# A masked attention kernel: the group-0 and group-1 setup in plain order, the last group's scores between its value products

## The chip, the cores and the metric

The kernel runs on one core of a Trainium2 chip. The metric is the device time of one execution in microseconds; the time before is the median of three runs. The profile comes from one further execution of the same program.

## The reference

For each of 128 matrices x[b] (128 nodes by 512 features) two layers are computed, with one 128 by 128 matrix adj for all:

```
h  = relu(layernorm(x))
A  = adj @ h[b]
x  = x + max over features of relu(A[:, None, :] + (A + b0 - A)[:, :, None])   # one number per node
h  = relu(layernorm(x))
q, k, v = h @ Wq + bq, h @ Wk + bk, h @ Wv + bv      # 8 heads of 64
w  = softmax(q k^T / 8 + mask(adj == 0))              # per head
x  = x + w @ v
```

The number that layer 0 adds is the same along a node's features, so that the second layernorm sees the same h; the kernel computes h once.

## The kernel before, in words

**Tiles and groups.** The 128 matrices are taken in 32 groups of 4. For each matrix `m`, `norm(m)` and `norm_end(m)` (lines 249 to 273) compute h in tile `hn`: VectorE (DVE) takes the statistics (`st`, `mv`, `ve`), GpSimd (POOL) the reciprocal deviation (`rstd`, line 264), DVE subtracts the mean and clips (line 269), ScalarE (ACT) scales (line 272), and POOL adds the value bias `bv_sb` to x (line 273). `adjacency(m)` (line 302) is one TensorE product of 512 columns with the transposed adj, and a DVE maximum over it (line 307), which gives the layer-0 number `C`. The transposed h goes to tile `hT` of its group: in groups 0 and 1 by four TensorE transposes and an ACT copy (`transposes`, line 295), in the later groups by a DVE transposition in blocks (`blocks`) and 16 small DMAs (`move`).

**Projections.** q, k and v of a group are computed by Winograd's form of Strassen's method: class `Products` (line 344) has seven methods p1 to p7, each with four matmuls of 256 columns on sums of weight blocks (`s1` to `s4`, made once by `weight_sum`) and of blocks of h (`t1` to `t4`, made by `h_sum`, four DVE instructions a group). Results leave the PSUM banks by ACT (`biased`) or DVE (`add`).

**Attention of one matrix.** `scores(g, i)` (line 471) are 8 products into a PSUM tile `sc` of which there is one, and two exponentials on ACT. `masks(w)` (line 488) are two DVE multiplications. `finish(g, i, w)` (line 492) are 16 products of weights and values into the PSUM tile `pav` (one buffer), whose 65th column is the sum of the weights; then, on DVE, the reciprocal of the sums into `RS`, the multiplication (line 508), and the sum with x and C (line 512); SyncE (SP) issues the output's DMA.

**Order.** Everything inside `tc.manual_schedule()` is ordered by hand. The main loop (lines 556 to 582) runs over the 128 matrices: scores of matrix b, then a share of the products of the next group (`products`, line 455: the last v product p3 of the present group comes in the first share), with masks, the norm of matrix b + 10, and `h_sum` of the group after next dealt in between, then `adjacency` and `finish`. The last group has no products to run beside but its own last one, so its four matrices are worked one after the other.

**The beginning** (lines 524 to 555). The four matrices of group 0 are normalised and transposed. q of group 0 is computed plainly (`plain_q`, 32 matmuls), its first half ahead of the last matrix's transposes. Then follow the 13 products of k and v, and after each product a piece of group 1 or of the first two matrices of group 2: norm and norm_end after one, transposes and adjacency (in the tiles `sc` and `pav`) after the next. Weight sums of k run on DVE, of v and q on POOL. x of group 0 and the weights are loaded in halves on SP's and ACT's queues in turn, x first.

**The end** (lines 585 to 594). After the loop all 1024 reciprocals of each partition are checked against two limits in two DVE passes, the second with a running sum `cnt`; one small product adds the partitions, and the sum goes to `flag`. Each engine loads `flag`, and the program branches to a slow general path if a number is out of range.

Of the kernel before, what the change touches and what calls it, by code (L numbers as in the profile page):

```python
# [36 lines left out]
F32 = mybir.dt.float32  # L41
I32 = mybir.dt.int32
AF = mybir.ActivationFunctionType
ALU = mybir.AluOpType
# [4 lines left out]
G = 4  # L49
# [113 lines left out]
def tile_adj_preln_d2(  # L163
# [36 lines left out]
    def fast(ctx):  # L200
# [6 lines left out]
        ps_sc = ctx.enter_context(tc.tile_pool(name="ps_sc", bufs=1, space=PSUM))  # L207
        ps_av = ctx.enter_context(tc.tile_pool(name="ps_av", bufs=1, space=PSUM))

        X, HN, TB, HT, HB, QT, KT, C, AMAX, WA, RSTD, MV, PR = ({} for _ in range(13))  # L210

        def load(g):
# [5 lines left out]
                )  # L218

        nc.scalar.dma_start(adj_sb, adj)  # L220
        X[0] = xpool.tile([P, G, N], F32, name="xg")
        for i in range(G):
            (nc.sync, nc.scalar)[i % 2].dma_start(X[0][:, i, :], x[i])
        for name, src in (("q", wq), ("k", wk), ("v", wv)):
            for h in range(2):
                (nc.sync, nc.scalar)[h].dma_start(
                    W[name][:, 2 * h : 2 * h + 2, :],
                    src[2 * h * P : (2 * h + 2) * P].rearrange("(c p) f -> p c f", p=P),
                )
        nc.gpsimd.dma_start(b0_sb, b0.rearrange("(p o) -> p o", o=1))  # L230
        nc.gpsimd.dma_start(bq_sb, bq.rearrange("(c p) -> p c", p=P), allow_slow_non_contiguous=True)
        nc.gpsimd.dma_start(bk_sb, bk.rearrange("(c p) -> p c", p=P), allow_slow_non_contiguous=True)
# [9 lines left out]

        pt = ps_mm.tile([P, 512], F32, name="mm")
        nc.tensor.transpose(pt[:, :D], adj_sb, ident)
        nc.scalar.copy(adjT, pt[:, :D])
        nc.vector.tensor_single_scalar(live, adjT, 0.0, op=ALU.not_equal)
        live_h = live.unsqueeze(1).to_broadcast([P, NC, D])

# [45 lines left out]

        def transposes(m):
            g, i = divmod(m, G)
            ph = ps_sc.tile([P, 2, NC, D], F32, name="sc")
            for c in range(NC):
                nc.tensor.transpose(ph[:, 0, c], HN[m][:, c * P : (c + 1) * P], ident)  # L299
            nc.scalar.copy(HT[g][:, i], ph[:, 0])  # L300

        def adjacency(m, pa=None):
            g, i = divmod(m, G)
            if pa is None:
                pa = ps_mm.tile([P, 512], F32, name="mm")
            nc.tensor.matmul(pa, adjT, HN[m], start=True, stop=True)  # L306
            nc.vector.reduce_max(AMAX[g][:, i : i + 1], pa, axis=AX.X)
            if i == G - 1:
                nc.vector.tensor_scalar(C[g], AMAX[g], b0_sb, 0.0, op0=ALU.add, op1=ALU.max)
# [13 lines left out]
                h_quarters(g)  # L323
            nc.vector.tensor_sub(HB[g][o], HB[g][a], HB[g][b])

        def weight_sum(eng, n, k):

            if k == 0:
                w = W[n]
                WA[n] = dict(  # L330
                    a11=w[:, 0:2, 0:HT2], a21=w[:, 0:2, HT2:N],
                    a12=w[:, 2:4, 0:HT2], a22=w[:, 2:4, HT2:N],
                    **{f"s{j + 1}": WS[n][:, j] for j in range(4)},
                )
            o, a, op, b = ("s1 a21 + a22", "s2 s1 - a11", "s3 a11 - a21", "s4 a12 - s2")[k].split()
            eng.tensor_tensor(
                WA[n][o], WA[n][a], WA[n][b], op=ALU.add if op == "+" else ALU.subtract
            )

        def weight_sums(eng, n):  # L340
            for k in range(4):
                weight_sum(eng, n, k)

        class Products:

# [86 lines left out]
                self.mm(self.c, "s4", "b22")  # L432
                self.add(self.dst(0, 1), self.c, self.u2)

        def plain_q(t):

            if t == 0:
                QT[0] = proj.tile([P, NC, T], F32, name="qT")
            h = HT[0][:, 2 * t : 2 * t + 2]
            for f in range(2):  # L440
                bank = ps_mm.tile([P, 2, HT2], F32, name="mm")
                for r in range(2):
                    k = 2 * f + r
                    for c in range(NC):
                        nc.tensor.matmul(  # L445
                            bank[:, r, :], W["q"][:, c, k * P : (k + 1) * P], h[:, :, c],
                            start=r == 0 and c == 0, stop=r == 1 and c == NC - 1,
                            skip_group_check=True,
                        )
                    nc.scalar.activation(  # L450
                        QT[0][:, k, t * HT2 : (t + 1) * HT2], bank[:, r], AF.Identity,
                        bias=bq_sb[:, k : k + 1],
                    )

        def products(g):


# [10 lines left out]
                (k.p3, v.p6, v.p2, v.p7, v.p5, v.p4),  # L468
            )

        def scores(g, i):

            psc = ps_sc.tile([P, 2, NC, D], F32, name="sc")
            for f in range(NC):
                for j in range(2):
                    r = slice(j * HD, (j + 1) * HD)
                    nc.tensor.matmul(  # L477
                        psc[:, j, f, :],
                        KT[g][r, f, i * D : (i + 1) * D],
                        QT[g][r, f, i * D : (i + 1) * D],  # L480
                        start=True, stop=True,
                    )
            w = work.tile([P, 2, NC, D], F32, name="w")
            for j in range(2):
                nc.scalar.activation(w[:, j], psc[:, j], AF.Exp, scale=HD ** -0.5)  # L485
            return w
# [2 lines left out]
            for j in range(2):  # L489
                nc.vector.tensor_tensor(w[:, j], w[:, j], live_h, op=ALU.mult)  # L490

        def finish(g, i, w):
            b = g * G + i
            pav = ps_av.tile([P, 2, 512], F32, name="pav")

            for h in range(H):
                for k in range(2):
                    r = slice(k * HD, (k + 1) * HD)
                    nc.tensor.matmul(  # L499
                        pav[r, h // 4, (h % 4) * HE : (h % 4 + 1) * HE],  # L500
                        w[:, h % 2, h // 2, r], V[g % 2][:, i, h, :],
                        start=True, stop=True,
                    )
            po = pav[:, :, 0 : 4 * HE].rearrange("p k (h e) -> p k h e", e=HE)
            rs = RS[:, b].rearrange("p (k h) -> p k h", k=2)
            nc.vector.reciprocal(rs, po[:, :, :, HD])
            o = work.tile([P, 2, 4, HD], F32, name="o")
            nc.vector.tensor_tensor(  # L508
                o, po[:, :, :, 0:HD], rs.unsqueeze(3).to_broadcast([P, 2, 4, HD]), op=ALU.mult
            )  # L510
            y = o.rearrange("p k h d -> p (k h d)")
            nc.vector.scalar_tensor_tensor(  # L512
                y, X[g][:, i, :], C[g][:, i : i + 1], y, op0=ALU.add, op1=ALU.add
            )
            nc.sync.dma_start(out[b], y)

        with tc.manual_schedule():
            def early(m):

                transposes(m)  # L520
                adjacency(m, ps_av.tile([P, 2, 512], F32, name="pav")[:, 0])


            for m in range(G):
                norm(m)
                norm_end(m)
                if m > 0:
                    early(m - 1)
            plain_q(0)
            early(G - 1)  # L530
            weight_sums(nc.vector, "k")
            for k in range(4):
                h_sum(0, k)
            plain_q(1)
            weight_sums(nc.gpsimd, "v")
            _, k, v = PR[0] = [None] + [Products(0, n) for n in "kv"]
            for s, p in enumerate((
                k.p1, k.p6, k.p2, k.p7, k.p5, k.p4, v.p1, k.p3, v.p6, v.p2, v.p7, v.p5, v.p4,
            )):
                p()  # L540
                m = G + s // 2
                if m < 2 * G + 2:
                    if s % 2 == 0:
                        norm(m)
                        norm_end(m)
                    elif m < 2 * G:
                        early(m)
                    else:
                        blocks(m)
                        adjacency(m, ps_av.tile([P, 2, 512], F32, name="pav")[:, 0])  # L550
                if s >= 4 and s % 2 == 0 and s < 12:
                    weight_sum(nc.gpsimd, "q", s // 2 - 2)
                if s >= 8 and s < 12:
                    h_sum(1, s - 8)
            move(2 * G + 1)
            for b in range(B):
                g, i = divmod(b, G)
                m = b + 2 * G + 2
                if i == 0 and g + 3 < NG:
# [22 lines left out]
                    move(m)  # L582


            ok = work.tile([P, 2, NC, D], F32, name="w").rearrange("p j f d -> p (j f d)")
            cnt = stat.tile([P, 1], F32, name="cnt")
            rs_all = RS.rearrange("p b h -> p (b h)")
            nc.vector.tensor_single_scalar(ok, rs_all, SUM_LO, op=ALU.is_ge)
            nc.vector.scalar_tensor_tensor(
                ok, rs_all, SUM_HI, ok, op0=ALU.is_le, op1=ALU.mult, accum_out=cnt  # L590
            )
            pc = ps_mm.tile([P, 512], F32, name="mm")
            nc.tensor.matmul(pc[0:1, 0:1], cnt, ones, start=True, stop=True)
            nc.vector.tensor_copy(flag, pc[0:1, 0:1])

    with ExitStack() as c:
        fast(c)
# [35 lines left out]
```

## Time and profile before

| | us |
|---|---|
| median of 3 runs (1621.72 to 1622.07) | 1621.97 |
| profiled execution, its own time | 1621.72 |
| its span, first to last instruction | 1620.0 |
| TensorE busy | 1586.6 |
| VectorE busy | 1114.2 |
| ScalarE busy | 422.9 |
| GpSimd busy | 259.6 |
| first scores start (after the beginning) | 74.97 |
| last product of the last v starts | 1595.60 |
| flag written | 1617.2 |

How to read it: the span is divided into the beginning, up to the first scores, the main loop, and the end, from the scores of the last matrix but four. Busy time counts instructions in execution, and a wait is idle time with a releaser in brackets behind the instruction that ends it. In the timeline each row has the start, the duration, engine, line, operation, output and inputs, and the count of merged instructions; an fp32 matmul has two records.

### The profile page before, as it was taken

Reading aid. Unit: us, or ns where it says so; the run is one execution under the profiler, and the core shown is the slowest. Engines: PE = TensorE matmul, PEld = TensorE weight load, DVE = VectorE, ACT = ScalarE, POOL = GpSimd, SP = SyncE. Lnnn points to the kernel's source line nnn. Section 1 sums busy time; section 2 is a strip of 40 time slices with the busy share of each in tenths; the row PEclk is TensorE's granted clock in tenths of the full one; section 3 lists DMA queues with packets and bytes.
Section 4 is the critical chain, followed back from the end, with each engine's and each line's share of the span. In section 5 each row is a group of like instructions: output and inputs, shape, how many; then the busy total and the mean of one; then the engine's idle time right before and its main releaser. Section 6 shows DMA issues by size and latency. Waiting matters only on the chain.

```text
span 1620.0 us, 29469 instructions
## 1 busy us (share of the span) xinstructions
PE 1586.6 (98%) x11819; PEld 1319.8 (81%) x11819; DVE 1114.2 (69%) x2044; ACT 422.9 (26%) x844; POOL 259.6 (16%) x278
## 2 busy tenths in 40 slices
PE   6899999999999999999999999999999999999996
PEld 4688888888888888888888888888888888888885
DVE  3576777766777767777767777667777677777655
ACT  2322222222222222222222222222222222222221
POOL 4311111111111111111111111111111111111000
PEclk9999999999999999999999999999999999999999
DMA  4033222232222232222332222322222322223201
GB/s 164 1 72 73 68 60 51 69 75 69 63 46 70 69 79 65 67 44 69 72 73 68 54 56 69 76 68 64 47 69 69 79 65 67 44 69 73 47 27 40
DMA packets 299082, 104.02 MB, mean 64 GB/s; under 512 B 264448, under 2 KB 264576, under 8 KB 298944
## 3 DMA queue, kind: packets, MB, share of 16 engines
q1 hardware_dynamic: 297520, 99.69, 25.5%
q8 instruction: 94, 1.54, 0.4%
q10 hardware_dynamic: 1248, 2.16, 0.4%
q14 instruction: 44, 0.36, 0.1%
q0 software_dynamic: 176, 0.27, 0.1%
HBM read 37.03 MB, written 33.55 MB: 44 GB/s over the span
## 4 chain that ended last, share of the span: by engine, by line
PE 97%; DVE 1%; ACT 1%; issue 0%; DMA 0%; POOL 0%; ACTq 0%; DVEq 0%; POOLq 0%
PE mm L372 72%; PE pav L499 9%; PE sc L477 8%; PE mm L306 6%; PE mm L445 1%; PE pav L306 1%; PE sc L299 0%; DVE w L490 0%; DMA xg<-in_x_dram 0%; ACT hn L272 0%; DVE o L512 0%; DVE o L508 0%; POOL rstd L264 0%; DVE st L259 0%; ACT qT L450 0%
## 5 line engine op out<-in xcount | busy, mean ns | idle before, releaser
L264 POOL TENSOR_TENSOR rstd<-ve,mhalf 128x1 f32<-128x1 f32 x128 | 84.3, 659 | 1225.9 <-DVE ve L262 1087.6
L485 ACT ACTIVATE w<-sc 128x512 f32<-128x512 f32 x256 | 138.9, 595 | 515.4 <-PE sc L477 515.4
L499 PEld LDWEIGHTS pav<-v,w 128*64 128x64 f32 x4096 | 130.3, 137 | 99.6 <-issue 54.4
L372 PE MATMUL mm<-hs,sq_sb 128*128 128x256 f32 x744 | 179.0, 383 | 0.0
L372 PE MATMUL mm<-hs,sk_sb 128*128 128x256 f32 x768 | 176.4, 379 | 0.0
L372 PE MATMUL mm<-sv_sb,hs 128*128 128x256 f32 x768 | 176.2, 379 | 0.0
L273 POOL TENSOR_TENSOR xg<-xg,bv_sb 128x512 f32<-128x512 f32 x128 | 162.9, 1273 | 35.2 <-DVE hn L269 27.5
L490 DVE TENSOR_TENSOR w<-w,live 128x512 f32<-128x512 f32 x256 | 164.7, 685 | 1.0 <-ACT w L485 1.0
L372 PEld LDWEIGHTS mm<-sv_sb,hs 128*128 128x128 f32 x768 | 145.9, 190 | 20.7 <-issue 1.0
L272 ACT ACTIVATE hn<-hn,rstd 128x512 f32<-128x512 f32 x128 | 92.9, 726 | 267.7 <-DVE hn L269 206.3
L372 PEld LDWEIGHTS mm<-hs,sk_sb 128*128 128x128 f32 x768 | 145.9, 190 | 20.3 <-issue 0.5
L372 PEld LDWEIGHTS mm<-hs,sq_sb 128*128 128x128 f32 x744 | 138.8, 190 | 21.4
L499 PE MATMUL pav<-v,w 128*64 128x65 f32 x4096 | 148.5, 224 | 6.7 <-DVE w L490 6.7
L477 PE MATMUL sc<-qT,kT 64*128 64x128 f32 x2048 | 148.7, 285 | 0.0
L420 DVE TENSOR_TENSOR u<-mm,p1b 128x512 f32<-128x512 f32 x63 | 43.5, 691 | 128.3 <-PE mm L372 128.3
L477 PEld LDWEIGHTS sc<-qT,kT 64*128 64x128 f32 x2048 | 124.2, 187 | 9.1 <-issue 0.3
L372 PE MATMUL mm<-hT,wk_sb 128*128 128x256 f32 x512 | 124.2, 385 | 0.0
L372 PE MATMUL mm<-wv_sb,hT 128*128 128x256 f32 x512 | 120.9, 379 | 0.0
L306 PE MATMUL mm<-hn,adjT 128*128 128x512 f32 x236 | 120.5, 592 | 0.0
L372 PE MATMUL mm<-hT,wq_sb 128*128 128x256 f32 x496 | 120.4, 386 | 0.0
L372 PEld LDWEIGHTS mm<-wv_sb,hT 128*128 128x128 f32 x512 | 97.3, 190 | 13.7 <-issue 0.5
L372 PEld LDWEIGHTS mm<-hT,wk_sb 128*128 128x128 f32 x512 | 94.7, 190 | 15.8 <-issue 0.5
(84 smaller groups left out, 2033.1 us busy)
## 6 DMA issues: line engine op xcount, KB each, us to landing
out_dram<-o SPq DMA_DIRECT2D x128, 256.0 KB, 2.1
xg<-in_x_dram SPq DMA_DIRECT2D x62, 512.0 KB, 5.1
hT<-tb SPq DMA_DIRECT2D x960, 32.0 KB, 2.0
xg<-in_x_dram SPq DMA_DIRECT2D x2, 256.0 KB, 3.4
xg<-in_x_dram ACTq DMA_DIRECT2D x2, 256.0 KB, 5.6
wq_sb<-in_L_gnn_Wq_dram SPq DMA_DIRECT2D x1, 512.0 KB, 7.9
wk_sb<-in_L_gnn_Wk_dram SPq DMA_DIRECT2D x1, 512.0 KB, 11.1
wq_sb<-in_L_gnn_Wq_dram ACTq DMA_DIRECT2D x1, 512.0 KB, 10.6
```

Source lines behind the costliest of these rows:

```text
L264: nc.gpsimd.tensor_tensor(rstd, ve, mhalf, op=ALU.pow)
L272: nc.scalar.activation(HN[m], HN[m], AF.Copy, scale=RSTD[m])
L273: nc.gpsimd.tensor_tensor(X[g][:, i, :], X[g][:, i, :], bv_sb, op=ALU.add)
L306: nc.tensor.matmul(pa, adjT, HN[m], start=True, stop=True)
L372: nc.tensor.matmul(bank[:, r, :], lhs, rhs, start=first and r == 0 and c == 0, stop=r == 1 and c == 1, skip_group_check=True,)
L420: nc.vector.tensor_tensor(self.u3, self.b, self.pf[1], op=ALU.add)
L445: nc.tensor.matmul(bank[:, r, :], W["q"][:, c, k * P : (k + 1) * P], h[:, :, c], start=r == 0 and c == 0, stop=r == 1 and c == NC - 1, ski ...
L477: nc.tensor.matmul(psc[:, j, f, :], KT[g][r, f, i * D : (i + 1) * D], QT[g][r, f, i * D : (i + 1) * D], start=True, stop=True,)
L485: nc.scalar.activation(w[:, j], psc[:, j], AF.Exp, scale=HD ** -0.5)
L490: nc.vector.tensor_tensor(w[:, j], w[:, j], live_h, op=ALU.mult)
L499: nc.tensor.matmul(pav[r, h // 4, (h % 4) * HE : (h % 4 + 1) * HE], w[:, h % 2, h // 2, r], V[g % 2][:, i, h, :], start=True, stop=True,)
```

## The change

It does two things. The beginning: x of group 0 is loaded by `load(0)` on SP in two transfers, each weight matrix in one transfer of 1 MB on ACT. The copy of the transposed adj moves from ACT to DVE. `plain_q` goes; q of group 0 is computed by `Products` as in all groups, and its weight sums run on DVE, those of k and v on POOL. The work of a group stands together: four matrices, `h_sum`, and for group 0 then all 20 products of q, k, v but the last; group 1's norms, transposes and adjacencies follow after these, then the two matrices of group 2. Transposes and adjacencies use the tile `mm` of the products.

The end: the main loop stops five matrices early. The last matrix of group 30 and the four of group 31 follow by hand, with the scores of group 31 between the last v products. Two of the weight tiles and one tile `pav` come from buffers that are free by then (`spare`). The check of the reciprocals is made in two parts by `count`: one over the first 124 matrices behind `finish` of matrix 3 of group 30, one over the last four at the end, whose small products add up in one PSUM tile.

```diff
-        X[0] = xpool.tile([P, G, N], F32, name="xg")
-        for i in range(G):
-            (nc.sync, nc.scalar)[i % 2].dma_start(X[0][:, i, :], x[i])
+        load(0)
         for name, src in (("q", wq), ("k", wk), ("v", wv)):
-            for h in range(2):
-                (nc.sync, nc.scalar)[h].dma_start(
-                    W[name][:, 2 * h : 2 * h + 2, :],
-                    src[2 * h * P : (2 * h + 2) * P].rearrange("(c p) f -> p c f", p=P),
-                )
+            nc.scalar.dma_start(W[name], src.rearrange("(c p) f -> p c f", p=P))
...
-        nc.scalar.copy(adjT, pt[:, :D])
+        nc.vector.tensor_copy(adjT, pt[:, :D])
...
         def transposes(m):
-            ph = ps_sc.tile([P, 2, NC, D], F32, name="sc")
+            ph = ps_mm.tile([P, NC, D], F32, name="mm")
...
-        def adjacency(m, pa=None):
+        def adjacency(m):
             g, i = divmod(m, G)
-            if pa is None:
-                pa = ps_mm.tile([P, 512], F32, name="mm")
+            pa = ps_mm.tile([P, 512], F32, name="mm")
...
+        def spare_tile():
+
+            t = proj.tile([P, NQ, 2, NC, Q], F32, name="tb")
+            return t.rearrange("p a i c r -> p (a i c r)")
+
-        def scores(g, i):
+        def scores(g, i, spare=False):
...
-            w = work.tile([P, 2, NC, D], F32, name="w")
+            if spare:
+                w = spare_tile().rearrange("p (j f d) -> p j f d", j=2, f=NC)
+            else:
+                w = work.tile([P, 2, NC, D], F32, name="w")
...
-            pav = ps_av.tile([P, 2, 512], F32, name="pav")
+            if spare:
+                pav = ps_sc.tile([P, 2, NC, D], F32, name="sc").rearrange("p j f d -> p j (f d)")
+            else:
+                pav = ps_av.tile([P, 2, 512], F32, name="pav")
...
+        def count(b0, b1):
+
+            r = RS[:, b0:b1].rearrange("p b h -> p (b h)")
+            ok = spare_tile()[:, 0 : (b1 - b0) * H] if b0 == 0 else live[:, 0 : G * H]
+            cnt = stat.tile([P, 1], F32, name="cnt")
+            nc.vector.tensor_single_scalar(ok, r, SUM_LO, op=ALU.is_ge)
+            nc.vector.scalar_tensor_tensor(
+                ok, r, SUM_HI, ok, op0=ALU.is_le, op1=ALU.mult, accum_out=cnt
+            )
+            if b0 == 0:
+                PC.append(ps_mm.tile([P, 512], F32, name="mm"))
+            nc.tensor.matmul(PC[0][0:1, 0:1], cnt, ones, start=b0 == 0, stop=b1 == B)
...
-            for m in range(G):
-                norm(m)
-                norm_end(m)
-                if m > 0:
-                    early(m - 1)
-            plain_q(0)
-            early(G - 1)
-            weight_sums(nc.vector, "k")
-            for k in range(4):
-                h_sum(0, k)
-            plain_q(1)
-            weight_sums(nc.gpsimd, "v")
-            _, k, v = PR[0] = [None] + [Products(0, n) for n in "kv"]
-            for s, p in enumerate((
-                k.p1, k.p6, k.p2, k.p7, k.p5, k.p4, v.p1, k.p3, v.p6, v.p2, v.p7, v.p5, v.p4,
-            )):
-                p()
-                m = G + s // 2
-                if m < 2 * G + 2:
-                    if s % 2 == 0:
-                        norm(m)
-                        norm_end(m)
-                    elif m < 2 * G:
-                        early(m)
-                    else:
-                        blocks(m)
-                        adjacency(m, ps_av.tile([P, 2, 512], F32, name="pav")[:, 0])
-                if s >= 4 and s % 2 == 0 and s < 12:
-                    weight_sum(nc.gpsimd, "q", s // 2 - 2)
-                if s >= 8 and s < 12:
-                    h_sum(1, s - 8)
+            for g in (0, 1):
+                for m in range(g * G, g * G + G + 1):
+                    if m < g * G + G:
+                        norm(m)
+                        norm_end(m)
+                    if m > g * G:
+                        transposes(m - 1)
+                        adjacency(m - 1)
+                for k in range(4):
+                    h_sum(g, k)
+                if g == 0:
+                    weight_sums(nc.vector, "q")
+                    weight_sums(nc.gpsimd, "k")
+                    weight_sums(nc.gpsimd, "v")
+                    PR[0] = q, k, v = [Products(0, n) for n in "qkv"]
+                    for p in (
+                        q.p1, q.p6, q.p2, q.p7, q.p5, q.p4, k.p1, k.p6, q.p3, k.p2, k.p7,
+                        k.p5, k.p4, v.p1, k.p3, v.p6, v.p2, v.p7, v.p5, v.p4,
+                    ):
+                        p()
+            for m in (2 * G, 2 * G + 1):
+                norm(m)
+                norm_end(m)
+                blocks(m)
+                adjacency(m)
             move(2 * G + 1)
-            for b in range(B):
+            for b in range(B - G - 1):
...
-            ok = work.tile([P, 2, NC, D], F32, name="w").rearrange("p j f d -> p (j f d)")
-            cnt = stat.tile([P, 1], F32, name="cnt")
-            rs_all = RS.rearrange("p b h -> p (b h)")
-            nc.vector.tensor_single_scalar(ok, rs_all, SUM_LO, op=ALU.is_ge)
-            nc.vector.scalar_tensor_tensor(
-                ok, rs_all, SUM_HI, ok, op0=ALU.is_le, op1=ALU.mult, accum_out=cnt
-            )
-            pc = ps_mm.tile([P, 512], F32, name="mm")
-            nc.tensor.matmul(pc[0:1, 0:1], cnt, ones, start=True, stop=True)
-            nc.vector.tensor_copy(flag, pc[0:1, 0:1])
+            g = NG - 1
+            k3, v6, v2, v7, v5, v4 = parts[G - 1]
+            w = scores(g - 1, G - 1)
+            k3()
+            masks(w)
+            v6()
+            w0 = scores(g, 0)
+            v2()
+            masks(w0)
+            finish(g - 1, G - 1, w)
+            count(0, B - G)
+            v7()
+            w1 = scores(g, 1)
+            v5()
+            masks(w1)
+            w2 = scores(g, 2, spare=True)
+            v4()
+            w3 = scores(g, 3, spare=True)
+            finish(g, 0, w0)
+            masks(w2)
+            PR[g][2].p3()
+            finish(g, 1, w1)
+            masks(w3)
+            finish(g, 2, w2, spare=True)
+            finish(g, 3, w3)
+            count(B - G, B)
+            nc.vector.tensor_copy(flag, PC[0][0:1, 0:1])
```

## The prediction

> **What bounds the kernel now.** I read the page first (engines, the 40 slices, the chain of work that ended last), then the busy time by stretch, then the timelines of the first 75 us and of the last 40 us.
>
> ```profile
> PE 1586.6 (98%) x11819; PEld 1319.8 (81%) x11819; DVE 1114.2 (69%) x2044; ACT 422.9 (26%) x844; POOL 259.6 (16%) x278
> PE   6899999999999999999999999999999999999996
> PE 97%; DVE 1%; ACT 1%; issue 0%; DMA 0%; POOL 0%; ACTq 0%; DVEq 0%; POOLq 0%
> ```
>
> The busy time of one stretch, the columns being stretch, length, then PE, PEld, DVE, ACT, POOL, clock, DMA share and GB/s:
>
> ```profile
> 118.90:1536.00 1417.10, 1417.10 (x10622) 1182.73 (x10620) 1002.82 (x1837) 374.19 (x750) 220.56 (x229) 1.00 0.27 65
> ```
>
> TensorE is full from 75 us to 1597 us: in the stretch of 1417.10 us it is busy 1417.10. The change leaves that loop alone, so only the two ends can move. Of TensorE's 33 us of idle time some 20 lie before 75 us and some 13 after 1597.6 us.
>
> The beginning, from the timeline (start, duration, then the work):
>
> ```profile
> 8.56 1.91 PE L306 MATMUL pav<-hn,adjT 128*128 128x512 f32 x2
> 12.11 1.26 POOL L273 TENSOR_TENSOR xg<-xg,bv_sb 128x512 f32<-128x512 f32 x1 [6.42 <-DVE mv L260]
> 15.34 1.11 PE L299 MATMUL sc<-ident,hn 128*128 128x128 f32 x4 [4.87 <-ACT hT L300]
> ...
> 44.89 0.68 DVE L259 BATCH_NORM_STATS2 st<-xg 128x6 f32<-128x512 f32 x1
> ...
> 46.06 0.73 POOL L264 TENSOR_TENSOR rstd<-ve,mhalf 128x1 f32<-128x1 f32 x1 [6.88 <-DVE ve L262]
> 46.76 1.26 POOL L273 TENSOR_TENSOR xg<-xg,bv_sb 128x512 f32<-128x512 f32 x1
> 46.82 0.72 ACT L272 ACTIVATE hn<-hn,rstd 128x512 f32<-128x512 f32 x1
> ...
> 47.60 0.66 PE L299 MATMUL sc<-ident,hn 128*128 128x128 f32 x4
> ...
> 48.09 1.02 PE L306 MATMUL pav<-hn,adjT 128*128 128x512 f32 x2
> ```
>
> The chain from the statistics to the transposes runs over three engines and takes 47.60 - 44.89 = 2.71 us. Here it lies beside products. POOL's 6.42 us before 12.11 are put down to DVE, which had long been done; what came last is the load of `bv_sb` (issued at 3.50, 8.5 us to landing). It holds the second `rstd`, hence the second matrix.
>
> The end:
>
> ```profile
> 1613.12 0.21 DVE L506 RECIPROCAL RS<-pav 128x8 f32<-128x8 f32 x1 [1.14 <-PE pav L499]
> 1613.37 0.69 DVE L508 TENSOR_TENSOR o<-pav,RS 128x512 f32<-128x512 f32 x1
> 1614.16 0.75 DVE L512 SCALAR_TENSOR_TENSOR o<-xg,c,o 128x512 f32<-128x512 f32 x1
> 1614.83 0.69 DVE L588 TENSOR_SCALAR w<-RS 128x1024 f32<-128x1024 f32 x1
> 1615.55 1.22 DVE L589 SCALAR_TENSOR_TENSOR w<-RS,w 128x1024 f32<-128x1024 f32 x1
> 1616.70 0.08 DVE L589 DVE_READ_ACCUMULATOR w<-RS,w 128x1 f32 x1
> 1616.84 0.09 PEld L593 LDWEIGHTS mm<-ones,cnt 128*1 128x1 f32 x2 [3.90 <-DVE w L589]
> ```
>
> From the last value product to the count's matmul it is 3.72 us, all DVE, while TensorE waits. The clock column shows what an idle TensorE costs:
>
> ```profile
> 1613.00:1613.20 0.20, 0.08 (x4) 0.00 (x0) 0.07 (x1) 0.00 (x0) 0.00 (x0) 1.00 0.00 0
> 1613.40:1613.60 0.20, 0.00 (x0) 0.00 (x0) 0.20 (x1) 0.00 (x0) 0.00 (x0) 0.50 0.00 0
> ```
>
> [...] 0.50 at 1613.3, and in the first 19 us an adjacency (two records) takes 1.71 us in the chain against 0.86 later, four transposes 1.11 against 0.65. [...] the trace shows no matmul out of the written order. [...] Here the loads keep them at 380 to 390 GB/s until about 20 us, so dealing x and weights over two queues moves an order, not the total.
>
> **The change part by part: beginning.** Written order per engine is kept in the hand-ordered part; I count on that. Times are from the span's start, a product (4 matmuls, 8 records) is 1.73 us.
>
> Group 0 as now up to the second matrix, because `bv_sb` still gates it. Its landing is the unknown: between 5.7 us (POOL would not stop: -6.4) and 20 us (end of all loads: +8); I take 12.1 again, the bytes being the same. With the weights alone on ACT's queue and x alone on SP's, each x pair lands later than now by an estimate of 1 to 3 us; the second pair is first read at 11 us, so that is hidden. The adjacency's transpose is copied on DVE (0.24 us, DVE idle there): nothing. Transposes into an `mm` bank no longer wait for the copy `hT` at 14.72: the second starts at 14.87 instead of 15.34 (-0.47). The fourth matrix's normalisation ends at 20.99, its transposes and adjacency at 22.55.
>
> q.p1 then runs to 24.28. q.p6 needs t2 and s2, and on DVE these stand behind one another: reduction and c 0.87, four `h_sum` 2.53, two weight sums 1.33 (from 30.12 to 36.05 now), so 22.60 + 4.73 = 27.33. TensorE idles 3.1 us. From 27.37, 19 products take 32.8: E = 60.2. (Plain q was 32 matmuls, Winograd's 28; that is in the sum.) The k and v sums on POOL end at about 31.6, before they are read.
>
> Group 1's norms, until now between these products, stand in DVE's queue behind the last eviction. From E: eviction 0.65, chain 2.71, transposes and adjacency 1.51: 4.87. The third matrix waits for the first's reduction: 0.64 + 2.64 + 1.51 = 4.79. The fourth comes 2.17 later, paced by POOL (0.7 + 1.27 each). Reduction, c and four `h_sum`: 3.32. Matrix 8: 2.77 + 0.86 = 3.63; its reduction 0.64; matrix 9: 3.63. Sum 23.05: the first scores start at 83.25, now 75.04. **+8.2 us** at full clock. Nothing covers this stage: no products are left to run in it. The loads and moves for later groups stay in place relative to the scores.
>
> **End.** I count from t = 0, the scores of matrix 3 of group 30 (1581.78 now). Scores 1.09, k.p3, v.p6, scores(31,0) 1.09, v.p2, finish 1.08: TensorE ends at 8.45; DVE is through with the masks by 8.2. Then count(0, 124). Its matmul is written before v.p7, so v.p7 and all behind it wait for reciprocal, two output steps and two passes over 992 numbers: 3.72 us less 0.05, plus 0.2 for itself. v.p7 starts at 12.45. Then v.p7, scores(31,1), v.p5, scores(31,2), v.p4, scores(31,3) to 20.91, finish(31,0) to 21.99, v.p3 to 23.72. The exponentials fit between the scores in one `sc` buffer (1.1 us against 1.73). From 22.05 DVE sets the end: three output steps 1.64, masks 1.24, v.p3's sum 0.65, steps 1.7, masks 1.24, steps 1.7 and 1.7, short count 0.5, matmul and flag 0.45: about 33.0. Now the flag is written at 35.43: **-2.4 us**. The gain without the stall would be 6.2. Unknown is whether the last output's landing (2.0 us after issue) shows beyond the program's last 2.8 us: 0 to +0.9; I take 0.
>
> **Clock restarts.** One restart cost 1.85 us at the start now (0.46 + 0.85 + 0.20 + 0.34 over the four pieces from 15.34 to 20.22). New idle stretches: before q.p6 3.1 us ([...] half, 0.9); E to the first transposes 3.4 us (1.3 on the chain); matrix 8 after 6 us idle (0.85); matrix 9 with the scores behind it (1.85); v.p7 after 3.8 us idle (1.85). Together **+6.75**, from 0 to about 12.
>
> Sum: 8.2 - 2.4 + 6.75 = +12.55. On the profiled run's 1621.72 (span 1620.0 and 1.7 around it) that is 1634.3; on the median of the three runs, 0.25 higher, 1634.5.
>
> **Rivals.**
> - The clock holds: [...] the end's rounds with 1.68 us idle in 4.15 kept 1.00. For it: those rounds. Against: 0.50 came at once [...]. 8.2 - 2.4: 1627.8.
> - More waits: group 1's stage stays at half clock (about +3), `bv_sb` lands later (+2), the finish of matrix 1 waits for v.p3's sum because it takes V as a whole (+2). For it: nothing in the stage fills TensorE over half. Against: nothing in the trace asks for all three. 1641.5.
> - The count's matmul holds nothing (another order): -6.2 in place of -2.4 and no restart there: 1628.9. Against: program order.
> - Faster than before: DVE does not keep the written order and starts group 1's norms in its idle time beside group 0's products. The stage of 23.05 would shrink to its matmuls, 7.8 us: -15.2, and its restarts (4.0) go: 1615.3. It decides once some 13 of these 19 us are taken in. For it: one copy written ahead of the ordered part (`adjT`, 7.50) ran behind a later normalisation on ACT. Against: inside that part every DVE and POOL instruction stands as written.
>
> **How the numbers follow.** Forecast 0.65, clock holds 0.13, more waits 0.12, count holds nothing 0.06, faster 0.04. The range, 1626.5 to 1641, takes in the forecast's restarts from nothing to about 12 us, the cases of the held clock and of the count, and reaches to the edge of the case of more waits. 0.2% is 3.2 us, about what can be told from no change: faster 0.04, same 0.04 (low ends of the clock and count cases), slower 0.92.
>
> **What would show it.** First scores at 83 to 88 us; products closed up from 27 to 60; transposes of group 1 after 60 with TensorE half idle and the clock at 0.50 in places; in the end a TensorE idle of 3.7 us released by the count's DVE pass, and slower v.p7. It is wrong if group 1's statistics run before 55 us, if the second matrix is released much before 14 us, or if the first scores come before 80.

## The result, and the profile after

The changed kernel takes 1644.08 us, median of 4 runs (1642.44 to 1644.41), beside 1622.02 us for the kernel before: the ratio is 1.0134, 95% interval [1.0117, 1.0152]. It is slower, as forecast, but by 22 us where the forecast had 12.5. The profiled execution took 1644.07 us, its span is 1642.2.

From the page of the changed kernel: TensorE's share and instructions among the engines, then its busy tenths and its clock, also in tenths, in the 40 slices.

```profile
PE 1592.8 (97%) x11813; PEld 1322.6 (81%) x11813; DVE 1124.5 (68%) x2053; ACT 421.3 (26%) x841; POOL 262.4 (16%) x278
PE   4879999999999999999999999999999999999997
PEclk8989999999999999999999999999999999999998
```

TensorE has six instructions fewer than before and is busy 6.2 us longer, so part of its work ran slowly. The slices that lost are the first and the third, 6-8-9 before and 4-8-7 now, and the clock, at 9 in every slice before, is 8 in both.

| us | before | after | difference |
|---|---|---|---|
| first scores start | 74.97 | 96.39 | +21.42 |
| from there to the scores of matrix 3 of group 30 | 1506.81 | 1507.50 | +0.69 |
| from there to the flag | 35.28 | 35.15 | -0.13 |
| from there to the end of the span | 2.94 | 3.16 | +0.22 |
| span | 1620.0 | 1642.2 | +22.2 |

So nearly all of it is in the beginning. The 0.69 us behind it are the first scores themselves, which took 1.87 us in place of 1.16. The timeline of the beginning after the change, in rows of start, duration, engine, line, operation, output and inputs:

```profile
24.71 0.68 DVE L317 TENSOR_TENSOR hs<-hT 128x512 f32<-128x512 f32 x1
...
26.98 1.74 DVE L317 TENSOR_TENSOR hs<-hT 128x512 f32<-128x512 f32 x1
28.14 1.70 POOL L324 TENSOR_TENSOR sv_sb<-wv_sb 128x512 f32<-128x512 f32 x1
...
33.87 3.75 PE L358 MATMUL mm<-hs,sq_sb 128*128 128x256 f32 x8 [8.85 <-DVE sq_sb L325]
...
70.52 0.68 DVE L253 BATCH_NORM_STATS2 st<-xg 128x6 f32<-128x512 f32 x1
...
73.22 0.66 PE L293 MATMUL mm<-ident,hn 128*128 128x128 f32 x4 [3.34 <-ACT hn L266]
...
88.89 2.07 PE L299 MATMUL mm<-hn,adjT 128*128 128x512 f32 x2 [6.21 <-ACT hn L266]
```

Two things are to be seen. q.p6 waits 8.85 us for a weight sum of DVE, and the DVE passes ahead of it last 1.74 us, though the first of the same kind took 0.68. POOL's passes beside them last 1.70 us, and the two engines start theirs in turn. And group 1's transposes and adjacencies, which in the kernel before lay between products, stand alone behind them, most of them with a wait for the normalisation.

The busy time by stretch, in the columns of the prediction, for the stretch of q.p6 and q.p2 and for group 1's stage:

```profile
33.80:40.40 6.60, 6.53 (x17) 5.30 (x18) 2.89 (x3) 0.00 (x0) 1.05 (x1) 0.54 0.00 0
69.90:96.40 26.50, 11.66 (x30) 4.33 (x30) 16.79 (x37) 6.34 (x10) 11.45 (x12) 0.77 0.00 1
```

In the first TensorE is full, but its granted clock is 0.54, and q.p6 and q.p2 take 6.49 us where two products at full clock take 3.46: nearly half of this time is lost to the clock. In the second it has 11.66 us of work in 26.50, at a clock of 0.77.

The end of the changed kernel, from its timeline:

```profile
1616.52 0.19 PE L505 MATMUL mm<-ones,cnt 128*1 128x1 f32 x2 [3.71 <-DVE tb L500]
1616.64 3.63 PE L358 MATMUL mm<-sv_sb,hs 128*128 128x256 f32 x8
```

The first count's small product waits 3.71 us for DVE, v.p7 stands behind it, and then v.p7 takes 3.63 us in place of 1.9, at a granted clock of 0.57 (1616.3 to 1620.3).

### The profile page after: what moved, and what is told of

Same layout as the page of the kernel before. It is cut to its first block, busy times and chain, and to the rows that moved or that the text cites. A ratio compares the mean times of both kernels' runs of the same rounds, so it can differ in the third digit from the quotient of the medians.

```text
span 1642.2 us, 29462 instructions
## 1 busy us (share of the span) xinstructions
PE 1592.8 (97%) x11813; PEld 1322.6 (81%) x11813; DVE 1124.5 (68%) x2053; ACT 421.3 (26%) x841; POOL 262.4 (16%) x278
## 4 chain that ended last, share of the span: by engine, by line
PE 94%; issue 3%; DVE 1%; POOL 1%; ACT 0%; DMA 0%; DVEq 0%; POOLq 0%; ACTq 0%
PE mm L358 70%; PE sc L448 9%; PE pav L476 8%; PE mm L299 7%; DMA xg<-in_x_dram 0%; ACT hn L266 0%; PE mm L293 0%; POOL rstd L258 0%; DVE o L485 0%; DVE amax L300 0%; DVE st L253 0%; DVE o L489 0%; DVE hs L317 0%; DVE tb L464 0%; POOL xg L267 0%
## 5 line engine op out<-in xcount | busy, mean ns | idle before, releaser
L358 PE MATMUL mm<-hs,sq_sb 128*128 128x256 f32 x768 | 186.4, 386 | 8.9 <-DVE sq_sb L325 8.9
L358 PEld LDWEIGHTS mm<-hs,sq_sb 128*128 128x128 f32 x768 | 144.4, 191 | 31.6 <-issue 9.2
L299 PE MATMUL mm<-hn,adjT 128*128 128x512 f32 x256 | 136.1, 614 | 9.6 <-ACT hn L266 9.6
L358 PE MATMUL mm<-hT,wq_sb 128*128 128x256 f32 x512 | 125.4, 388 | 0.0
L300 DVE TENSOR_REDUCE amax<-mm 128x1 f32<-128x512 f32 x128 | 86.1, 673 | 53.7 <-PE mm L299 52.9
L358 PEld LDWEIGHTS mm<-hT,wq_sb 128*128 128x128 f32 x512 | 95.7, 192 | 16.3 <-issue 0.5
```

The source lines that it names most:

```text
L358: nc.tensor.matmul(bank[:, r, :], lhs, rhs, start=first and r == 0 and c == 0, stop=r == 1 and c == 1, skip_group_check=True,)
```

## The experiments

Times are compared with runs of the kernel before on the same chip, whose medians lay between 1622.5 and 1623.1, so "+14.2" means 14.2 us over that. Single runs of the kernel before lay between 1620.95 and 1626.27, so a difference in the medians under about 1 us says nothing. The changed kernel stands at +22.1 in this count. The expectations name kernels by their time or by a short name: e1_sums_apart is the first below, e2_end_alone the end alone, e4_total_late the changed kernel with the first count's product moved.

**The two engines' sums apart.** In the changed kernel POOL's k and v sums wait, by one small addition, for DVE's last q sum.

```diff
                     weight_sums(nc.vector, "q")
+                    gate = stat.tile([P, 1], F32, name="ve")
+                    nc.gpsimd.tensor_tensor(
+                        gate, WS["q"][:, 3, 1, N // 2 - 1 : N // 2], mhalf, op=ALU.add
+                    )
                     weight_sums(nc.gpsimd, "k")
```

> The changed kernel, with one tiny POOL addition put ahead of POOL's k and v weight sums that reads the last of DVE's q weight sums, so that POOL's sums run after DVE's instead of beside them. [...] DVE's sums of two SBUF tensors and POOL's take turns while both run, and that alone makes the six DVE passes between 24.7 and 33.7 us cost 8.9 instead of 3.9 us; apart, the passes take 0.68 each, q.p6 starts at 28.3 to 28.8 instead of 33.87, and the time falls by 5 to 6.5 us, to 1637.5 to 1639. Rival operands: the passes are slow because of what they read (hT just written, weight blocks); then they stay at 1.7 us and the time at 1644.

Measured 1637.25 us, +14.2, ratio 1.0085 [1.0067, 1.0103]; first scores at 89.18. Its timeline, a DVE pass, q.p6 and the first pass of POOL:

```profile
25.20 0.68 DVE L317 TENSOR_TENSOR hs<-hT 128x512 f32<-128x512 f32 x1
...
27.96 2.80 PE L358 MATMUL mm<-hs,sq_sb 128*128 128x256 f32 x8 [3.26 <-DVE sq_sb L325]
...
29.24 1.26 POOL L324 TENSOR_TENSOR sk_sb<-wk_sb 128x512 f32<-128x512 f32 x1
```

All eight DVE passes are back at 0.68 to 0.69 and POOL's at 1.26 to 1.27, and the wait at q.p6 is 3.26 us, near the 3.1 that the prediction had. Delaying POOL's work by 7 us made the kernel 7 us faster. The sizes fit passes that take turns: the 1.74 us of a DVE pass are its own 0.68 and most of one of POOL's, 1.26. That the two engines slow each other is shown here; why they do, no run tests.

**The same collision put into the kernel before.** There POOL's v sums ran from 21.89 to 26.94 beside matmuls, and DVE's eight passes from 30.99. A like addition makes POOL start with DVE.

```diff
+            gate = stat.tile([P, 1], F32, name="ve")
+            nc.gpsimd.tensor_tensor(gate, C[0][:, 0:1], mhalf, op=ALU.add)
             weight_sums(nc.gpsimd, "v")
```

> The kernel before with POOL's v weight sums held back, by a tiny POOL addition ahead of them that reads C of group 0, until DVE makes its k weight sums and h sums (31 to 36 us): the disputed collision by itself. [...] DVE's eight passes of 0.68 and POOL's four of 1.26 alternate, about 1.7 us for each pair while POOL has work; DVE is through at 40 to 41 instead of 36.05, the norm of matrix 4 and k.p6 follow later, and the time rises by 2 to 4.5 us. Rival operands: passes stay at 0.68, time unchanged.

Measured 1623.0 us, +0.5, ratio 1.0001 [0.9991, 1.001]. The timeline:

```profile
37.28 1.72 POOL L336 TENSOR_TENSOR sv_sb<-wv_sb,sv_sb 128x512 f32<-128x512 f32 x1
37.79 1.75 DVE L324 TENSOR_TENSOR hs<-hT 128x512 f32<-128x512 f32 x1
39.58 0.69 DVE L324 TENSOR_TENSOR hs<-hT,hs 128x512 f32<-128x512 f32 x1
```

The slowing appears in another kernel with other tiles and goes in the pass after POOL's last one. DVE was through 5.3 us later (41.39 instead of 36.05), 1.0 of it because the whole chain began later in this profile (31.15 instead of 30.12), and the time didn't rise: plain q's products ran meanwhile, and k.p6, which reads the sums, was not held. The transposes of matrix 4 waited 0.87 us in place of 0.54, and the first scores, at 76.40, were 1.4 us later than before, of which 1.0 was there from the start. So the slowing is confirmed and its expected price is not: the collision cost time where someone waited for the sums (8.85 us at q.p6 in the changed kernel, 3.26 with the sums apart), and none that can be told where nobody did (+0.5 here).

**Group 1 laced between products again,** in the changed kernel.

```diff
+                p()
+                t = s - 2
+                m = G + t // 2
+                if 0 <= t and m < 2 * G + 2:
+                    if t % 2 == 0:
+                        norm(m)
+                        norm_end(m)
+                    elif m < 2 * G:
+                        early(m)
...
+                if 8 <= t < 12:
+                    h_sum(1, t - 8)
```

> The changed kernel with the norms, transposes, adjacencies and sums of group 1 and of matrices 8 and 9 dealt between group 0's products again, as the kernel before deals them (from q.p2 on, with its PSUM tiles); loads, Winograd q, weight sums and the end as changed. Theory: the stage of 26.6 us between the last v product and the first scores goes and leaves its 7.8 us of matmuls: first scores at about 77.5 instead of 96.4, time 1644.1 - 18.8 = 1625.3, or up to 3 more where a norm comes late for its place. Rival: the stage is mostly work that TensorE has to do anyway; then under 10 us are gained, 1634 or more.

Measured 1633.14 us, +10.1, ratio 1.0057 [1.0039, 1.0075]; first scores at 84.90. That lies between the two forecasts: the first scores are 11.5 us earlier, not 18.8. The transposes and adjacencies now wait for their norms, with 1.62, 0.54, 2.09, 1.75 and 1.68 us of idle TensorE, and the collision is still whole, with q.p6 at 33.25:

```profile
33.25 3.75 PE L359 MATMUL mm<-hs,sq_sb 128*128 128x256 f32 x8 [8.85 <-DVE sq_sb L326]
...
60.49 0.66 PE L513 MATMUL sc<-ident,hn 128*128 128x128 f32 x4 [2.09 <-ACT hn L266]
```

**Both cures at once,** the two edits above in one kernel. Six matrices are laced, not the eleven of the expectation: the four of group 1 and matrices 8 and 9.

> The changed kernel with both cures of its beginning: POOL's k and v weight sums held back until DVE's q sums are through, and the eleven matrices of group 1 interleaved with group 0's products as before. Theory "two separate losses" (the sums of the two engines slow each other, 6.8 us when taken alone; the unlaced beginning leaves TensorE short and idle, 11 us when taken alone): they add, 1644.1 - 6.8 - 11 = 1626.3 us, first scores at about 78. Rival "one loss seen twice" (with the order laced, the late norms set the pace whichever way the sums go): no better than the laced order alone, 1633 us, first scores at about 85.

Measured 1633.93 us, +11.4, ratio 1.0068 [1.0051, 1.0084]; first scores at 87.03. The rival's number: all that the parted sums had brought is lost again. The timeline of this kernel shows where it went:

```profile
31.63 0.15 DVE L256 TENSOR_SCALAR ve<-mv 128x1 f32<-128x1 f32 x1
...
38.27 1.26 POOL L328 TENSOR_TENSOR sv_sb<-wv_sb,sv_sb 128x512 f32<-128x512 f32 x1
39.49 0.55 POOL L258 TENSOR_TENSOR rstd<-ve,mhalf 128x1 f32<-128x1 f32 x1
...
40.08 0.72 ACT L266 ACTIVATE hn<-hn,rstd 128x512 f32<-128x512 f32 x1 [7.49 <-POOL rstd L258]
...
40.85 1.11 PE L513 MATMUL sc<-ident,hn 128*128 128x128 f32 x4 [7.42 <-ACT hn L266]
```

The held sums are a block of 10.3 us on POOL, and the reciprocal deviation of matrix 4, ready to be worked out at 31.78, stands behind it until 39.49. The profile names ACT as the releaser of TensorE's 7.42 us; ACT was waiting for POOL.

**The sums dealt out behind the norms.**

```diff
-            weight_sums(nc.gpsimd, "k")
-            weight_sums(nc.gpsimd, "v")
...
+                if t in (0, 2):
+                    weight_sums(nc.gpsimd, "k", (t, t + 1))
+                if t in (4, 6, 8, 10):
+                    weight_sums(nc.gpsimd, "v", (t // 2 - 2,))
```

> The kernel with both cures (1633.9 us, first scores 87.03), with POOL's eight k and v sums dealt out behind the norms of group 1 rather than in one block ahead of them. Theory "the block on POOL holds the reciprocal deviation of matrix 4 from 31.8 to 39.5, so TensorE waits 7.4 us": that wait goes, first scores at 77 to 79, 1624 to 1626 us; the two cures add after all. Rival "late norms set the pace in any case": first scores at 84 to 87, 1631 to 1634 us.

Measured 1624.89 us (12 runs, 1621.97 to 1628.25), +2.0, ratio 1.0007 [0.9997, 1.0016], no longer told from the kernel before.

```profile
28.68 3.75 PE L364 MATMUL mm<-hs,sq_sb 128*128 128x256 f32 x8 [2.75 <-DVE sq_sb L329]
...
34.32 0.72 POOL L258 TENSOR_TENSOR rstd<-ve,mhalf 128x1 f32<-128x1 f32 x1 [4.31 <-DVE ve L256]
...
36.24 1.26 POOL L327 TENSOR_TENSOR sk_sb<-wk_sb 128x512 f32<-128x512 f32 x1
...
36.98 0.64 PE L518 MATMUL sc<-ident,hn 128*128 128x128 f32 x4
```

First scores came at 80.21 in the profiled execution, a little behind the 77 to 79 expected; it was the slowest of the 12, and in it q.p6 and q.p2 ran slowly (3.75 and 3.19 us, where the previous kernel's profile has 1.97 and 1.89; the first slice of its clock is at 8 tenths, there at 9). The deviation of matrix 4 no longer stands behind the sums, and its transposes start without a wait, which settles it: the two losses add, and the block on POOL had hidden it. Of the 22 us, some 8 go with the parted sums and some 12 more with the lacing.

**The clock kept up.** On the kernel with the sums apart, products of 512 columns that nobody reads are added in TensorE's idle stretches.

```diff
+            def keep(n):
+                t = ps_av.tile([P, 2, 512], F32, name="pav")
+                for _ in range(n):
+                    nc.tensor.matmul(t[:, 0], ident, W["q"][:, 0, :], start=True, stop=True)
...
+                        if p == q.p1:
+                            keep(4)
+                    keep(3)
...
+                keep(6 if m == 2 * G else 3)
```

> The kernel of e1_sums_apart with products that nobody reads (identity by a weight slice, 512 columns, 0.86 us each, into the idle tile pav) put into TensorE's idle stretches of the beginning: 4 behind q.p1, 3 behind v.p4, 6 ahead of matrix 8's adjacency, 3 ahead of matrix 9's. They fit in the idle time, so they only keep the clock up. Theory restarts: at half clock the beginning loses 1.8 us at q.p6 and q.p2, about 1.3 at group 1's first matrices, 0.85 at each of the adjacencies of matrices 8 and 9, 0.7 at the first scores: 5.5 below e1_sums_apart (1637.25), 1631.8. Rival: the stage of group 1 is paced by DVE, ACT and POOL alone; then only q.p6, q.p2 and the scores gain, 2.5 us, 1634.7.

Measured 1634.33 us, +11.8, ratio 1.0064 [1.0047, 1.0082]. First scores at 83.45, 5.73 earlier than without, 1.2 of it from an earlier q.p1. q.p6 took 1.96 us in place of 2.80, the adjacencies of matrices 8 and 9 1.12 in place of 2.07, the first scores 1.16 in place of 1.72, and the third slice of the clock is at 9 tenths in place of 8. So the restarts in the beginning were worth some 4.5 us. Group 1's stage took 23.7 us. The whole gained only 2.4 us: from the last count's product to the end of the span it was 6.3 us instead of 3.4. The waits and the page of this kernel show where:

```profile
SPq L636 <- PEq L607: 2.9, 1, 2.9
...
q8 instruction: 95, 1.56, 0.4%
```

SyncE's queue waits 2.9 us for TensorE's queue at the branch on `flag` (line 607), and q8, which the profile lists as an instruction queue, has 95 packets where it has 94 in the kernel before, the changed one and the one with the sums apart. This loss lies behind the last matmul (1624.99), so it isn't one of matmuls at a lower clock; whether the branch waited for that packet isn't shown. The total thus agrees with the rival's 1634.7 by luck; the 4.5 us ahead of the scores fit the theory, which had 4.8 there (5.5 less the 0.7 of the scores themselves).

**The loads alone,** in the kernel before.

```diff
-            (nc.sync, nc.scalar)[i % 2].dma_start(X[0][:, i, :], x[i])
+        load(0)
...
+            nc.scalar.dma_start(W[name], src.rearrange("(c p) f -> p c f", p=P))
```

> The kernel before with the changed kernel's loads of x of group 0 and of the weights (two transfers of x on SP, three of 1 MB on ACT), nothing else. Theory: bv_sb lands about 0.9 us later, as in the trace after (POOL's first addition at 13.00 instead of 12.11), and that shifts all behind it: +0.9, first scores at 75.9. Rival: the plain q products hide it, 0; or q waits for the one large transfer of wq (12.3 us to landing from 1.21, so 13.5, ahead of the products at 20): 0 too.

Measured 1623.07 us, +0.5, ratio 0.9999 [0.9992, 1.0006]. POOL's first use of `bv_sb` came at 12.42 and the first scores at 75.14, 0.2 us later than before. The way x and the weights are dealt over the queues costs nothing that can be told.

**The end alone,** the new end behind the old beginning.

```diff
-            for b in range(B):
+            for b in range(B - G - 1):
...
+            finish(g - 1, G - 1, w)
+            count(0, B - G)
+            v7()
```

> The beginning of the kernel before with the new end. Theory: the end is worth nothing as it stands (from the scores of matrix 3 of group 30 to the flag 35.15 us in the trace after, 35.28 before), so the time is 1621.9, within 0.5 of before, and the whole +22 is the beginning's. Rival: a part of the loss is the end's (the clock restart behind the count is larger than it looks), 1624 or more.

Measured 1623.29 us, +0.2, ratio 0.9995 [0.9986, 1.0004]: as expected nothing.

**The first count's product moved behind the last scores,** DVE's counting left in place, in the changed kernel.

```diff
-            count(0, B - G)
+            cnt = count(0, B - G)
...
             w3 = scores(g, 3, spare=True)
+            total(cnt, 0, B - G)
```

> The changed kernel with the first count's small matmul moved behind the last scores; the DVE passes stay where they are. Theory: the 3.7 us in which v.p7 waits for that matmul and the restart of 1.9 us behind it go, 1644.1 - 5.5 = 1638.6. Rival: DVE sets the end anyway, its passes being ahead of the evictions that v.p5 and the masks need; then 2 us or less, 1642 or more.

Measured 1638.24 us, +15.2, ratio 1.0088 [1.0071, 1.0105]. The timeline shows v.p7 at its own pace and the product with no wait:

```profile
1612.03 1.99 PE L358 MATMUL mm<-sv_sb,hs 128*128 128x256 f32 x8
...
1621.07 0.19 PE L508 MATMUL mm<-ones,cnt 128*1 128x1 f32 x2
```

The last count came 6.14 us earlier than in the changed kernel, 0.58 of it from its beginning: the stall with its restart is worth 5.6 us.

**That end with the old beginning.**

> The beginning of the kernel before, the new end, and the first count's small matmul moved behind the last scores: both repairs in one. Theory: as e4_total_late against the changed kernel (1638.24 against 1644.08), 5.8 us below e2_end_alone: 1617.3, and below the kernel before by 5.5. Rival: [...] the gain is under 3 us.

Measured 1617.3 us (1616.72 to 1617.92), -5.2, ratio 0.9957 [0.994, 0.9973]: faster than both kernels. Two more edits go on from there.

```diff
+        nc.gpsimd.dma_start(bv_sb, bv.rearrange("(o f) -> o f", o=1).to_broadcast([P, N]))
         nc.gpsimd.dma_start(b0_sb, b0.rearrange("(p o) -> p o", o=1))
...
-        nc.gpsimd.dma_start(bv_sb, bv.rearrange("(o f) -> o f", o=1).to_broadcast([P, N]))
```

> The beginning of the kernel before with the end's count held behind the last scores (1617.3 us), and in it the bias column bv_sb loaded first on POOL's queue instead of last. Theory "the place in the queue sets when it lands": bv_sb lands at 7 to 9 us instead of 12, the second matrix's chain and everything behind it 4 to 4.5 us earlier, 1613 us. Rival [...] it lands as late as before, first scores at 75 to 76, 1617 us. Worse if the columns now landing later (the other biases, the mask) hold the first matrix.

Measured 1613.3 us (1612.59 to 1614.03), -9.2, ratio 0.9943 [0.9927, 0.996]. POOL's first use of `bv_sb`, in the previous kernel and in this one:

```profile
11.96 1.26 POOL L274 TENSOR_TENSOR xg<-xg,bv_sb 128x512 f32<-128x512 f32 x1 [6.27 <-DVE st L260]
...
7.17 1.27 POOL L274 TENSOR_TENSOR xg<-xg,bv_sb 128x512 f32<-128x512 f32 x1 [1.54 <-DVE hn L270]
```

First scores moved from 75.78 to 72.44.

Then plain q's activations behind both halves of a bank:

```diff
+                for r in range(2):
+                    k = 2 * f + r
                     nc.scalar.activation(
```

> The previous kernel with plain q's two activations of a bank issued after both halves of the bank rather than after each half, which should remove four waits of TensorE of 0.56 us in the first products. Theory: 2.2 us below the previous kernel, about 1611 us. Rival: the waits only move to the next bank or to the scores, no change.

Measured 1609.26 us (1609.03 to 1609.47), -13.2, ratio 0.992 [0.9903, 0.9937]. Plain q ran without a gap, 7.07 and 7.17 us for its two halves, and first scores came at 67.59. That is 4.85 us earlier. The four waits account for 3.3 of them: each was 0.56 us of idle time but 0.82 us from start to start. Another 1.3 are an earlier start of plain q, since the third matrix's transposes and adjacency ran faster in this profile (the transposes 0.66 us in place of 1.03, the adjacency 1.03 in place of 1.92). The edit changes nothing ahead of plain q, so that part is luck as far as the runs show; the four timed runs, 1609.03 to 1609.47, are all about 4 us below the previous kernel's median.

## Why the prediction was right in direction and wrong in size

Three lines of the kernel before bear on the step that failed:

```profile
12.12 1.53 DVE L269 TENSOR_SCALAR hn<-xg,mv 128x512 f32<-128x512 f32 x1
...
30.99 0.68 DVE L336 TENSOR_TENSOR sk_sb<-wk_sb 128x512 f32<-128x512 f32 x1
...
37.22 0.72 POOL L264 TENSOR_TENSOR rstd<-ve,mhalf 128x1 f32<-128x1 f32 x1 [10.28 <-DVE ve L262]
```

- **First scores at 83.25 plus restarts.** By its terms they belonged at 87.15 (0.9, and 3.0 of the stage's 4.0, ahead of the scores); they came at 96.39. The miss of 9.2 us is nearly the whole error in the total (1644.08 - 1634.5 = 9.6), and it divides as follows: 6.5 at the start of q.p6, 2.1 in the restart there, 0.5 in group 1's stage.
- **The step that failed** is the sum for q.p6: reduction and c, "four `h_sum` 2.53, two weight sums 1.33", "so 22.60 + 4.73 = 27.33". It took the durations from 30.12 to 36.05 of the kernel before, where POOL stood still, while the next lines of the prediction let the k and v sums run on POOL over the same stretch "before they are read". Measured 33.87. Of the 6.5 us, 5.6 are the collision (from the last reduction to q.p6 it is 10.54 us here and 4.95 in the kernel with the sums apart), 0.7 a later start of the chain and 0.2 the chain alone, which was summed a little short. The prediction costed POOL's sums at nothing because nobody needed their result; what they took was not a result but DVE's time (passes of 1.63 to 1.75 us in place of 0.68). The 0.68 us at 30.99 fall into POOL's idle 10.28 us ahead of 37.22. And there was a sign: at 12.12 one DVE normalisation took 1.53 us beside a POOL pass begun at 12.11, where it takes 0.48 alone.
- **Restart at q.p6, "half, 0.9".** Half a restart was the author's estimate, for 3.1 us of idle time. It was 8.85, and q.p6 and q.p2 took 6.49 us in place of 3.46, +3.0, with the granted clock at 0.50 from 33.87 to 37.30. That is 2.1 over the term. A 3.26 us gap alone already gave 2.80 + 2.78 us, so half was too little here, but the kernel with both cures has 1.97 + 1.89 after the same gap. From these profiles the term can't be had closer than 0 to 3. The 1.85 us of one restart were read from durations alone: from 7.6 to 22 us of the kernel before the clock column stands at 1.00, though two adjacencies took 1.91 us each there, where later ones take 1.02. In the changed kernel the column shows 0.50 beside the like: from 88.8 to 91.0 and from 94.3 to 96.4, where adjacencies took 2.07 and 2.08 us.
- **Group 1's stage, 23.05 and 3.0 of restarts.** Right: 26.5 measured, 23.7 with the clock kept up. That nothing covers it was right too. What lacing can win back was 11.5 to 12.2, not the whole: the stage's own matmuls remain, and the laced norms have waits of their own.
- **`bv_sb` at 12.1, loads nothing.** 13.0 measured, +0.9 in this profile; in other kernels with the same loads it was between 11.47 and 12.62, and the loads alone showed no loss. The 380 to 390 GB/s that the prediction reads up to 20 us hold from 12 us on (387, with the 16 DMA engines at a busy share of 1.05); from 8 to 12 it was 353.
- **The end, -2.4 and a restart of 1.85.** Right in each term: 3.71 us of wait where 3.72 was forecast, 3.63 us for v.p7. The prediction's sum for the start of v.p7 comes to 12.32 and not 12.45; measured from the same zero it is 12.75. Together -0.55 was forecast and -0.13 measured, and the end alone gave no change.
- **The rivals.** The clock didn't hold (0.54 at q.p6). "More waits", at 1641.5, came nearest in time, but by luck and not by its terms: group 1's stage wasn't 3 us over, `bv_sb` was 0.9 late and not 2, and the finish of matrix 1, at 1630.33, didn't wait for v.p3's sum, which starts at 1631.44. The count's product held v.p7 (3.71 us). DVE kept the written order: group 1's first statistics came at 70.52, behind the last eviction, so the faster case fell.

## What to carry to other kernels

Sums on GpSimd beside sums on VectorE are not free merely because nobody waits for GpSimd's result (5.6 us here): cost them in VectorE's chain, and take a duration only from a stretch where the same neighbours run. When work is pushed behind other work to part the two, list all that is queued behind it: a block of sums on GpSimd took back as much as parting it had saved (1633.93 us parted and laced, 1633.14 laced alone). Where an engine keeps the written order, as TensorE did here (v.p7 stood behind the count's product, which waited 3.71 us), a small product that needs a late result belongs behind the work that doesn't. And the load that is needed first is worth trying first on its queue (4.0 us here).

## What the runs showed of the hardware that was not expected

- Two-input fp32 passes of 128x512 on DVE went from 0.68 us to between 1.63 and 1.78, and POOL's from 1.26 to between 1.59 and 1.78, while both engines ran them, in three kernels (the changed one, the one with group 1 laced, and the kernel before with the collision). From start to start a pass alone took 0.60 us on DVE and 1.22 on POOL, and a pair of them together 1.67 (26.98 to 28.65): nearly the sum. Not every DVE operation is slowed: in the kernel with both cures the statistics at 30.70 took 0.68 us beside a POOL pass of 1.27, and in the one with the sums apart a pass that reads PSUM took 0.69 at 35.17 beside one of 1.26.
- The idle time after which TensorE ran slower isn't a sharp number: after 3.26 us before q.p6 one kernel had 2.80 and 2.78 us for the next two products and another 1.97 and 1.89; after 2.75 us a third had 3.75 and 3.19 (there the adjacency at 21.78 took 1.91 us in place of 1.02 and q.p1 2.45 in place of 1.89, so it had come back to full pace only about 4 us earlier). In the kernel before, the granted clock fell from 1.00 to 0.50 at 1613.3, about 0.2 us after the last value product; in the two rounds ahead, with the same gaps of 1.5 and 0.17 us, it had kept 1.00. What decides it these runs do not show, and up to 3 us in one place hang on it.
- A load's place among four small ones on POOL's queue moved its landing by much more than its issue: `bv_sb`, issued 2.2 us earlier, was used 4.8 us earlier (7.17), and 3.9 in the last kernel (8.03). From issue to landing it took 5.8 us in the first of the two, in the last kernel 6.8 from issue to use (1.27 to 8.03), and 7.8 to 9.4 to landing in the kernels that issue it last.
